# Another order for the closing steps of a graph attention layer on one Trainium2 core

## The chip, the cores and the metric

The kernel runs on one core of a Trainium2 chip. The metric is the device time of one execution in microseconds (us). For the kernel before it is 2030.86 us, the median of three runs (2030.07, 2030.86 and 2034.2). One further execution was profiled; it took 2036.32 us, of which its trace covers 2034.5 us.

## What is computed

The graph has 12500 nodes with 128 features and 200000 edges sorted by destination. Each destination keeps its 16 best edges.

```python
h = relu(layernorm(x))
score = einsum('md,md->m', (h @ W_Q.T)[dst], (h @ W_K.T)[src]) / sqrt(128) * exp(-edge_weight)
keep  = the 16 highest scores of each dst
alpha = softmax of the kept scores over the edges of one dst
agg   = segment_sum(alpha * (h[src] @ W_msg.T), dst)
out   = x + relu(h @ W_self.T + agg)
```

## The kernel before

**Groups.** The edges are cut into 112 groups of 14 chunks of 128 edges. Each group also looks one chunk into the next group, so it has 15 chunks; the last group, L = 111, has 9. All edges of a group point into a window of at most 128 destination nodes. A group goes through these steps, each a small function of the same name in the code:

- `q_to_edges(g, b)` (L596, TensorE): spreads the nodes' queries to the edges, block b of four chunks, in float32.
- `scores(g, b)` (L605, VectorE): one fused multiply and sum for each chunk, on the rows `hs` that GpSimd has gathered. `scores_in_slots` (L613, VectorE) puts the scores into 40 slots for each node.
- `slots_by_node` (L619, L621, TensorE), `slots_out` (L626, ScalarE), `node_by_slots` (L629, TensorE): the slots arrive with one node in each partition.
- `best` (L635 to L647, VectorE): nine small instructions that find the top 16 and leave them in `km`. `sum_of_exps` (L652, ScalarE) gives the softmax denominator.
- `kept_to_edges` (L664, TensorE): brings `km` back to the edges. `kept_on_edges` is `one_over_sum` (L657, L658, VectorE), `on_edges` (L670 to L677, VectorE: `up`, `mine`, `kept`) and `exps` (L681, ScalarE).
- `weights` (L685, L686, VectorE) writes the weight matrix `alz`.
- `sums(g, 0)` and `sums(g, 1)` (L696, TensorE): the weighted sums of the rows, the first half of the chunks and the rest: 7 and 8 chunks, 14 and 16 float32 matmul records. `sums_out` (L701, ScalarE) normalises them into `agn`; `sums_turned` and `sums_turned_out` (L704 on TensorE, L708 on ScalarE) transpose that.
- `products` (L711, L712, TensorE): the two weight products. `output` (L716, VectorE) applies relu and adds x. `store` writes the rows: through SyncE's queue (L722), and for the last four groups by an indirect DMA that GpSimd issues (L725).

**Order.** The order is written by hand. A schedule with no reordering is in force from the start of the loop over groups: every engine executes its own instructions in the order in which the program calls them, and waits on semaphores for those of other engines. Within the main loop the steps of six neighbouring groups are interleaved. The loop ends one iteration early, and a straight list of calls, the end's list, finishes the groups that are under way, L-5 to L. Only this list is changed.

**PSUM and buffers.** Three PSUM banks matter. `so` (tile `s` in the profile) holds four 128-column quarters: a transpose of h, the query, the transposed sums, and the result of `products`. `et` (tile `e`) holds slots and, inside the loop, the sums. Tile `a` holds the sums in the end's list. An engine's access to a bank waits for another engine's earlier access to the same bank, even if they touch different quarters: in the built program `sums_turned`, which writes one quarter of `so`, waits for the `output` called ahead of it, which reads another. A store waits for the stores before it, because all write `out`.

**Helpers of the end's list.** `turned(g)` is `sums_turned` and `sums_turned_out`; `all_slots(g)` is `slots_by_node` for three blocks and `slots_out`; `all_sums(g)` is both parts of `sums` and `sums_out`; `to_rows(g)` is `products`, `output` and `store`.

Of the kernel before, what the change touches and what calls it, by code (L numbers as in the profile page):

```python
# [20 lines left out]
P = 128  # L21
# [39 lines left out]
def bc(ap, n):  # L61

    return ap.unsqueeze(2).to_broadcast([ap.shape[0], ap.shape[1], n])


def upper(ap):

    return ap.bitcast(BF16).rearrange("p (n two) -> p n two", two=2)[:, :, 1]
# [8 lines left out]
def gnn_layer(  # L77
# [54 lines left out]
    def bank(tag, bufs):  # L132
        return psum.tile([P, 512], F32, tag=tag, bufs=bufs, name=tag)
# [376 lines left out]
    with tc.tile_pool(name="win", bufs=2) as win:  # L510
# [4 lines left out]
        def rows_of(g, j):  # L515
            return T[g]["hs"][:, j, :] if j < GC else T[g + 1]["hs"][:, 0, :]

        def start_of(g, row, most):
            return nc.values_load(row_i[0:1, row, g:g + 1], engines=[SP], min_val=0, max_val=most,
                                  skip_runtime_bounds_check_because="clamped above")  # L520
# [69 lines left out]
        def q_to_edges(g, b):  # L590
            j0, j1 = 4 * b, min(4 * b + 4, chunks[g])
            if j0 >= j1:
                return
            T[g]["pq", b] = pq = bank("q", 3)
            for j in range(j0, j1):
                nc.tensor.matmul(pq[:, (j - j0) * P:(j - j0 + 1) * P],  # L596
                                 lhsT=T[g]["to_e"][:, j * P:(j + 1) * P], rhs=T[g]["q"], start=True, stop=True)
# [30 lines left out]
        def node_by_slots(g):  # L628
            nc.tensor.transpose(et[:, 256:256 + KM + 1], T[g]["eT"], ident[0:KM + 1, 0:KM + 1])  # L629


        def best(g):
            pt = et[:, 256:256 + KM + 1]
            ell = win.tile([P, KM], F32, name="ell")
            nc.vector.tensor_scalar(ell, slots, pt[:, KM:KM + 1], NEG, op0=OP.is_ge, op1=OP.mult)  # L635
            nc.vector.tensor_add(ell, ell, pt[:, 0:KM])
            T[g]["v16"] = v16 = win.tile([P, TOPK], F32, name="v16")
            rest = win.tile([P, KM], F32, name="rest")
            nc.vector.max(v16[:, 0:8], ell)
            nc.vector.match_replace(rest, v16[:, 0:8], ell, NEG)  # L640
            nc.vector.max(v16[:, 8:16], rest)
            nc.vector.match_replace(rest, v16[:, 8:16], rest, NEG)
            T[g]["km"] = km = win.tile([P, KM + 3], F32, name="km")
            nc.vector.tensor_scalar(km[:, KM:KM + 1], v16[:, 0:1], FLOOR, -1.0, op0=OP.max, op1=OP.mult)
            nc.vector.tensor_tensor(km[:, 0:KM], rest, ell, op=OP.not_equal)
            for k in range(KM, KM + 2):
                nc.vector.tensor_sub(km[:, k + 1:k + 2], km[:, k:k + 1], upper(km[:, k:k + 1]))  # L647

        def sum_of_exps(g):
            T[g]["e16"] = win.tile([P, TOPK], F32, name="e16")  # L650
            T[g]["den"] = win.tile([P, 1], F32, name="den")
            nc.scalar.activation(T[g]["e16"], T[g]["v16"], AF.Exp, bias=T[g]["km"][:, KM:KM + 1],  # L652
                                 accum_out=T[g]["den"])

        def one_over_sum(g):
            T[g]["rden"] = rden = win.tile([P, 1], F32, name="rden", bufs=4)
            nc.vector.tensor_scalar(rden, T[g]["den"], 0.25, None, op0=OP.max)  # L657
            nc.vector.reciprocal(rden, rden)  # L658


        def kept_to_edges(g):
            T[g]["px"] = px = psum.tile([P, NJ + 1, 64], F32, tag="x", bufs=1, name="x")
            for j in range(chunks[g]):
                nc.tensor.matmul(px[:, j, 0:KM + 3], lhsT=upper(T[g]["to_e"][:, j * P:(j + 1) * P]),  # L664
                                 rhs=upper(T[g]["km"]), start=True, stop=True)
# [13 lines left out]
        def exps(g):  # L679
            n = chunks[g]  # L680
            nc.scalar.activation(T[g]["up"][:, 0:n], T[g]["up"][:, 0:n], AF.Exp)  # L681

        def weights(g):
            n, kept = chunks[g], T[g]["kept"]
            nc.vector.tensor_tensor(kept[:, 0:n], T[g]["up"][:, 0:n], kept[:, 0:n], op=OP.mult)  # L685
            nc.vector.tensor_tensor(alz[g % 2].rearrange("e (j w) -> e j w", w=WW + STEP)[:, 0:n, 0:WN],  # L686
                                    T[g]["ow"][:, 0:n, :], bc(kept[:, 0:n], WN), op=OP.mult)


        def sums(g, part, at=None):  # L690
            n = chunks[g]
            if part == 0:
                T[g]["pa"] = et[:, 384:384 + P] if at is None else at
            half = n // 2
            for j in range(half) if part == 0 else range(half, n):
                nc.tensor.matmul(T[g]["pa"], lhsT=alz[g % 2][:, WW * j + PRE:WW * j + PRE + P],  # L696
                                 rhs=rows_of(g, j), start=(j == 0), stop=(j == n - 1))

        def sums_out(g):
            T[g]["agn"] = win.tile([P, D], F32, name="agn")  # L700
            nc.scalar.activation(T[g]["agn"], T[g]["pa"], AF.Copy, scale=T[g]["rden"])  # L701

        def sums_turned(g):
            nc.tensor.transpose(so[:, 2 * P:3 * P], T[g]["agn"], ident)  # L704

        def sums_turned_out(g):
            T[g]["aggT"] = win.tile([P, P], F32, name="aggT")
            nc.scalar.copy(T[g]["aggT"], so[:, 2 * P:3 * P])  # L708

        def products(g):  # L710
            nc.tensor.matmul(so[:, 3 * P:4 * P], lhsT=T[g]["hT"], rhs=wselfT, start=True, stop=False)  # L711
            nc.tensor.matmul(so[:, 3 * P:4 * P], lhsT=T[g]["aggT"], rhs=wmsgT, start=False, stop=True)  # L712

        def output(g):
            T[g]["o"] = win.tile([P, D], F32, name="o")
            nc.vector.scalar_tensor_tensor(T[g]["o"], so[:, 3 * P:4 * P], 0.0, T[g]["x_t"],  # L716
                                           op0=OP.max, op1=OP.add)

        def store(g):

            if g < G - TAIL:
                nc.sync.dma_start(out[ds(start_of(g, 0, N - P), P), :], T[g]["o"])  # L722
            else:
                k = g - (G - TAIL)
                nc.gpsimd.indirect_dma_start(  # L725
                    out=out[:, :], out_offset=bass.IndirectOffsetOnAxis(ap=idxo[:, k:k + 1], axis=0),
                    in_=T[g]["o"], in_offset=None, bounds_check=N - 1, oob_is_err=False)
# [90 lines left out]
        L = G - 1  # L818
        blocks = -(-chunks[L] // 4)

        def turned(g):
            sums_turned(g)
            sums_turned_out(g)

        def all_sums(g):
            sums(g, 0, bank("a", 1)[:, 0:P])
            sums(g, 1)
            sums_out(g)

        def to_rows(g):  # L830
            products(g)
            output(g)
            store(g)

        def all_slots(g):
            for b in range(3):
                slots_by_node(g, b)
            slots_out(g)

        def kept_on_edges(g):  # L840
            one_over_sum(g)
            on_edges(g)
            exps(g)

        q_to_edges(L, 0)
        output(L - 5)
        store(L - 5)
        weights(L - 3)
        turned(L - 4)
        all_slots(L - 1)  # L850
# [2 lines left out]
        for b in range(1, blocks):  # L853
            q_to_edges(L, b)
        node_by_slots(L - 1)
        to_rows(L - 4)
        kept_to_edges(L - 2)
        all_sums(L - 3)
        scores(L, 0)
        kept_on_edges(L - 2)  # L860
        best(L - 1)
        sum_of_exps(L - 1)
        weights(L - 2)
        kept_to_edges(L - 1)
        scores(L, 1)
        turned(L - 3)
        all_sums(L - 2)
        for b in range(2, blocks):
            scores(L, b)
        scores_in_slots(L)  # L870
        all_slots(L)
        products(L - 3)
        node_by_slots(L)
        kept_on_edges(L - 1)
        weights(L - 1)
        output(L - 3)
        store(L - 3)
        best(L)
        sum_of_exps(L)
        turned(L - 2)  # L880
        pa = bank("a", 1)[:, 0:P]
        sums(L - 1, 0, pa)
        kept_to_edges(L)
        sums(L - 1, 1)
        sums_out(L - 1)
        to_rows(L - 2)
        kept_on_edges(L)
        weights(L)
        turned(L - 1)
        all_sums(L)  # L890
        to_rows(L - 1)
        turned(L)
        to_rows(L)
    assert not later
    order.close()

# [180 lines left out]
```

## Time and profile before

| What | Value |
|---|---|
| median of three runs | 2030.86 us |
| profiled execution | 2036.32 us |
| span of its trace | 2034.5 us |
| TensorE matmul busy | 1580.1 us (78%) |
| GpSimd busy | 1505.6 us (74%) |
| VectorE busy | 1284.9 us (63%) |
| ScalarE busy | 1021.7 us (50%) |
| mean granted TensorE clock | 0.915 |
| first steps that the change moves | 1991.75 us from the start |
| last gather issued (L176) | 1991.09 us |
| last store starts on GpSimd (L725) | 2021.33 us |

The shares of the whole span describe the main loop, 1990 us of it. The change concerns only the last 43 us, so the timeline of that stretch is what has to be read: one row for each instruction, or for a run of equal ones, with its start, its length, the engine, the line, the operands, and in brackets how long the engine sat idle ahead of it and which instruction ended that. PEld is TensorE's loading of weights, which overlaps its matmuls.

### The profile page before, as it was taken

What the parts mean: (1) busy time and instruction counts of PE and PEld (TensorE: products, weight loads), DVE (VectorE), ACT (ScalarE), POOL (GpSimd) and SP (SyncE); (2) the same over time, 40 slices, a digit from 0 to 9 for tenths busy, and PEclk for the clock granted to TensorE, in tenths of its full rate; (3) what the DMA queues carried; (4) which work ended last, traced back from release to release, by engine and by line L of the source; (5) the groups of instructions that cost most, each with busy time, mean ns of one, the idle gap of its engine ahead of it and who ended that gap; (6) DMA issues with size and microseconds to landing.
All of it is one profiled execution on the core that took longest, in us unless ns stands there. A gap on an engine that the chain in (4) does not pass through costs nothing. (4 is left out here: it accounts for less than half of the span.)

```text
span 2034.5 us, 42215 instructions
## 1 busy us (share of the span) xinstructions
PE 1580.1 (78%) x13800; PEld 1303.9 (64%) x13801; DVE 1284.9 (63%) x7017; ACT 1021.7 (50%) x2190; POOL 1505.6 (74%) x1580
## 2 busy tenths in 40 slices
PE   0268899977878787888878787778878787878785
PEld 0147777766666666666666666666666666666664
DVE  7568877756656666666666566666666665666653
ACT  5765566544444454454444445444544444545440
POOL 6777777777777777777777777777777777777772
PEclk9979999998889899998888899898988888989987
DMA  9522222222222222222222222222222222222220
GB/s 220 179 59 56 76 69 69 66 64 66 65 65 66 65 64 63 66 65 65 66 65 66 66 65 64 64 64 65 66 66 65 65 66 66 66 64 64 64 58 19
DMA packets 101472, 143.46 MB, mean 71 GB/s; under 512 B 31063, under 2 KB 74327, under 8 KB 100480
## 3 DMA queue, kind: packets, MB, share of 16 engines
q0 software_dynamic: 50144, 102.74, 19.9%
q1 hardware_dynamic: 51102, 37.99, 6.8%
q8 instruction: 108, 1.77, 0.4%
q14 instruction: 118, 0.97, 0.2%
HBM read 126.79 MB, written 14.40 MB: 69 GB/s over the span
## 5 line engine op out<-in xcount | busy, mean ns | idle before, releaser
L176 POOL DMA_INDIRECT hs<-h_tab,ix x1507 | 1436.4, 953 | 461.9 <-issue 304.6
L605 DVE SCALAR_TENSOR_TENSOR prod<-hs,dec_all,q 128x128 f32<-128x128 f32 x1674 | 507.6, 344 | 296.2 <-DMA hs<-h_tab,ix 256.8
L558 ACT ACTIVATE far<-a,minus 128x512 bf16<-128x512 f32 (+1 forms) x447 | 294.3, 658 | 530.8 <-PE a L556 523.7
L596 PE MATMUL q<-q,to_e 128*128 128x128 f32 x3348 | 512.4, 301 | 0.0
L596 PEld LDWEIGHTS q<-q,to_e 128*128 128x128 f32 x3348 | 482.6, 213 | 33.5 <-DVE prod L605 13.7
L696 PE MATMUL e<-hs,alz 128*128 128x128 f32 x3240 | 419.1, 282 | 0.0
L696 PEld LDWEIGHTS e<-hs,alz 128*128 128x128 f32 x3240 | 377.9, 192 | 26.9 <-issue 19.2
L581 ACT ACTIVATE aw<-a 128x400 bf16<-128x400 f32 x336 | 169.1, 503 | 314.3 <-PE a L579 314.3
L635 DVE TENSOR_SCALAR ell<-slots,e 128x40 f32<-128x40 f32 x112 | 28.1, 251 | 357.1 <-PE e L621 304.6
L704 PE MATMUL s<-ident,agn 128*128 128x128 f32 x112 | 38.3, 342 | 262.8 <-DVE kept L685 260.8
L563 ACT ACTIVATE to_e<-far 128x1920 f32<-128x1920 bf16 x112 | 201.4, 1798 | 3.5
L556 PE MATMUL a<-rel,ident 112*128 112x512 bf16 (+1 forms) x447 | 195.0, 436 | 8.2 <-ACT far L558 8.1
L704 PEld LDWEIGHTS s<-ident,agn 128*128 128x128 f32 x112 | 17.0, 152 | 279.0 <-issue 274.7
L621 PE MATMUL e<-opo,sl 128*41 128x40 f32 x3348 | 194.0, 233 | 0.0
L621 PEld LDWEIGHTS e<-opo,sl 128*41 128x41 f32 x3348 | 180.1, 147 | 12.3
L605 DVE DVE_READ_ACCUMULATOR prod<-hs,dec_all,q 128x1 f32 x1674 | 138.4, 83 | 0.0
L585 ACT ACTIVATE opo<-aw 128x1200 f32<-128x1200 bf16 x112 | 134.2, 1198 | 0.1
L191 DVE COPY ix<-idx_all 128x2 int32<-128x2 int32 x754 | 133.2, 192 | 0.0
L579 PE MATMUL a<-minus_at,pdT 32*128 32x400 bf16 x336 | 115.4, 343 | 19.3 <-ACT pdT L572 9.6
L664 PE MATMUL x<-km,to_e 128*128 128x43 bf16 x1674 | 61.1, 183 | 66.7 <-DVE km L647 66.0
L664 PEld LDWEIGHTS <-to_e 128*128 128x128 bf16 x1674 | 49.7, 97 | 98.3 <-DVE km L647 96.7
L613 DVE TENSOR_TENSOR sl<-opo,s 128x600 f32<-128x600 f32 x112 | 87.6, 782 | 4.0
(179 smaller groups left out, 1678.0 us busy)
## 6 DMA issues: line engine op xcount, KB each, us to landing
hs<-h_tab,ix POOLq DMA_INDIRECT x1507
h_r<-h_tab SPq DMA_DIRECT2D x112, 64.0 KB
x_t<-in_x_dram SPq DMA_DIRECT2D x108, 64.0 KB
out_dram<-o SPq DMA_DIRECT2D x108, 64.0 KB
xg<-in_x_dram SPq DMA_DIRECT2D x2, 1400.0 KB
h_tab<-xg SPq DMA_DIRECT2D x2, 1400.0 KB
xg<-in_x_dram SPq DMA_DIRECT2D x1, 1120.0 KB
h_tab<-xg SPq DMA_DIRECT2D x1, 1120.0 KB
```

The lines of the kernel that those rows point to most:

```text
L176: nc.gpsimd.indirect_dma_start(out=T[g]["hs"][:, j, :], out_offset=None, in_=table[0:N, :], in_offset=bass.IndirectOffsetOnAxis(ap=index(j ...
L191: nc.vector.tensor_copy(ix[:, j0:j1], idx_all[:, GC * g + j0:GC * g + j1])
L556: nc.tensor.matmul(pr[:, 0:n1 - n0], lhsT=upper(ident[0:RR, g:g + 1]).to_broadcast([RR, P]), rhs=rel[:, n0:n1], start=True, stop=True)
L558: nc.scalar.activation(T[g]["far"][:, n0:n1], pr[:, 0:n1 - n0], AF.Square, bias=minus)
L563: nc.scalar.activation(T[g]["to_e"][:, 0:n], T[g]["far"][:, 0:n], AF.Relu, bias=1.0, scale=-1.0)
L579: nc.tensor.matmul(pr[:, 0:400], lhsT=T[g]["pdT"], rhs=minus_at.rearrange("k w j s -> k (w j s)")[:, n0:n1], start=True, stop=True)
L581: nc.scalar.activation(T[g]["aw"][:, n0:n1], pr[:, 0:400], AF.Square)
L585: nc.scalar.activation(T[g]["opo"].rearrange("e w j s -> e (w j s)"), T[g]["aw"], AF.Relu, bias=1.0, scale=-1.0)
L596: nc.tensor.matmul(pq[:, (j - j0) * P:(j - j0 + 1) * P], lhsT=T[g]["to_e"][:, j * P:(j + 1) * P], rhs=T[g]["q"], start=True, stop=True)
L605: nc.vector.scalar_tensor_tensor(prod, rows_of(g, j), dec_all[:, c:c + 1], T[g]["pq", b][:, (j % 4) * P:(j % 4 + 1) * P], op0=OP.mult, op1 ...
L621: nc.tensor.matmul(et[0:KM + 1, STEP * j:STEP * j + WN], lhsT=sl1[g % 2][:, j, :], rhs=T[g]["ow"][:, j, :], start=False, stop=(j == n - 1))
L696: nc.tensor.matmul(T[g]["pa"], lhsT=alz[g % 2][:, WW * j + PRE:WW * j + PRE + P], rhs=rows_of(g, j), start=(j == 0), stop=(j == n - 1))
```

## The change

`all_sums` and `to_rows` are dissolved into their parts and the parts are called at other places of the end's list. No step is added or dropped. In the order of the list:

- `output(L-4)` and its store move from ahead of `scores(L, 0)` to behind `kept_on_edges(L-2)`.
- `sums_out(L-3)` moves behind `exps(L-2)` and `sum_of_exps(L-1)`.
- `sums(L-2, 1)` moves behind all of `slots_by_node(L)`; `sums_out(L-2)` moves behind `exps(L-1)`.
- `products(L-3)` moves behind `node_by_slots(L)`; `output(L-3)` and its store move from ahead of `best(L)` to behind it.
- `kept_on_edges(L)` moves ahead of `sums_out(L-1)`, `products(L-2)` and `output(L-2)`; the last comes behind `weights(L)`.

In the built program the number of waits differs by one, an extra instruction that only waits; everything ahead of the end's list is the same.

```diff
-        def all_sums(g):
+        def begun(g):
             sums(g, 0, bank("a", 1)[:, 0:P])
-            sums(g, 1)
-            sums_out(g)
-
-        def to_rows(g):
-            products(g)
-            output(g)
-            store(g)
...
+        def written(g):
+            output(g)
+            store(g)
+
         q_to_edges(L, 0)
-        output(L - 5)
-        store(L - 5)
+        written(L - 5)
         weights(L - 3)
         turned(L - 4)
         all_slots(L - 1)
...
         node_by_slots(L - 1)
-        to_rows(L - 4)
+        products(L - 4)
         kept_to_edges(L - 2)
-        all_sums(L - 3)
+        begun(L - 3)
+        sums(L - 3, 1)
         scores(L, 0)
         kept_on_edges(L - 2)
+        written(L - 4)
         best(L - 1)
         sum_of_exps(L - 1)
         weights(L - 2)
+        sums_out(L - 3)
         kept_to_edges(L - 1)
         scores(L, 1)
         turned(L - 3)
-        all_sums(L - 2)
+        begun(L - 2)
         for b in range(2, blocks):
             scores(L, b)
         scores_in_slots(L)
         all_slots(L)
-        products(L - 3)
+        sums(L - 2, 1)
         node_by_slots(L)
         kept_on_edges(L - 1)
+        sums_out(L - 2)
         weights(L - 1)
-        output(L - 3)
-        store(L - 3)
+        products(L - 3)
         best(L)
         sum_of_exps(L)
+        written(L - 3)
         turned(L - 2)
-        pa = bank("a", 1)[:, 0:P]
-        sums(L - 1, 0, pa)
+        begun(L - 1)
         kept_to_edges(L)
         sums(L - 1, 1)
+        kept_on_edges(L)
         sums_out(L - 1)
-        to_rows(L - 2)
-        kept_on_edges(L)
         weights(L)
+        products(L - 2)
+        written(L - 2)
         turned(L - 1)
-        all_sums(L)
-        to_rows(L - 1)
+        begun(L)
+        sums(L, 1)
+        sums_out(L)
+        products(L - 1)
+        written(L - 1)
         turned(L)
-        to_rows(L)
+        products(L)
+        written(L)
```

## The prediction

> **What bounds the kernel now.** I read first the chain of work that ended last, because the shares of the whole span (TensorE 78%, GpSimd 74%) belong to the main loop, which the change doesn't touch.
>
> ```profile
> 4 pieces in order of time: start us, us, what
> 2018.37 0.98 DMA out_dram<-o,idxo
> 2019.35 1.77 issue
> 2021.12 0.51 POOLq L904
> 2021.63 0.68 POOL out_dram L725
> ```
>
> The span ends with stores. The last one, store(L), starts 2.96 us after store(L-1) began, although its rows are there at 2020.14: it waits until the one before has landed. After its start at 2021.33 come 13.2 us in which no engine works; I take them as fixed. So the end is "start of store(L-1) + 2.96 + 13.2", and what counts is when output(L-1) is ready. Then I read the timeline of the last 45 us backwards from there.
>
> ```profile
> 2003.54 0.37 ACT L701 ACTIVATE agn<-a,rden 128x128 f32<-128x128 f32 x1 [5.13 <-PE a L696]
> 2004.47 0.26 ACT L626 COPY eT<-e 41x128 f32<-41x128 f32 x1 [0.57 <-PE e L621]
> 2004.88 0.17 DVE L685 TENSOR_TENSOR kept<-up,kept 128x15 f32<-128x15 f32 x1 [2.45 <-ACT up L681]
> 2005.99 0.24 DVE L635 TENSOR_SCALAR ell<-slots,e 128x40 f32<-128x40 f32 x1
> 2006.13 0.33 PE L704 MATMUL s<-ident,agn 128*128 128x128 f32 x1 [0.86 <-DVE o L716]
> 2010.90 0.29 DVE L716 SCALAR_TENSOR_TENSOR o<-s,x_t 128x128 f32<-128x128 f32 x1 [2.88 <-ACT agn L701]
> 2013.84 3.01 PE L696 MATMUL a<-hs,alz 128*128 128x128 f32 x18 [2.20 <-DVE alz L686]
> 2017.80 0.29 DVE L716 SCALAR_TENSOR_TENSOR o<-s,x_t 128x128 f32<-128x128 f32 x1 [4.01 <-PE s L712]
> ```
>
> From below: output(L-1) waits for products behind sums(L); sums(L) wait for the weights of L; these wait behind output(L-2) on VectorE, idle for 2.88 us. Above, VectorE stands 2.45 us for exps(L-1), which on ScalarE is queued behind sums_out(L-2) and eT(L), and so behind all 30 matmul records of sums(L-2). The last view is the busy time by microsecond; after the five engines stands the granted clock.
>
> ```profile
> 1996.00:1997.00 1.00, 0.00 (x0) 0.00 (x0) 0.90 (x9) 0.09 (x2) 0.00 (x0) 1.00 0.00 0
> 1999.00:2000.00 1.00, 1.00 (x7) 1.00 (x7) 0.96 (x7) 0.00 (x0) 0.00 (x0) 0.50 0.00 0
> 2009.00:2010.00 1.00, 1.00 (x12) 1.00 (x11) 0.00 (x0) 0.00 (x0) 0.00 (x0) 1.00 0.00 0
> 2016.00:2017.00 1.00, 1.00 (x6) 1.00 (x6) 0.00 (x0) 0.05 (x1) 0.00 (x0) 0.50 0.00 0
> ```
>
> After an idle stretch TensorE runs at half clock for about 3.4 us. At full clock 16 records of sums last 1.87 us (2008.32 to the next step at 2010.19), so 0.117 each; sums(L-2) ran at half clock from 1998.30 to 2001.47 and made its other 15 records by 2003.2 at that pace, so the first 15 cost 0.21 each.
>
> **The change part by part.** No step is added or removed, so every cost is a wait. Times are those of the trace; a step keeps its own length and its distance to the step that releases it. One distance isn't constant: from the end of a matmul to VectorE 0.04 to 0.10 us pass; I take 0.10.
>
> *output(L-4) off the front of scores(L,0).* VectorE ends `km` of L-2 at 1990.51 and idles 1.24 us for products(L-4). Now the four scores go at 1990.43 (the same step overlaps its forerunner by 0.08 at 1974.30) and last 4 x 0.27. Their rows are there: a gather issued at 1981.11 let its score go at 1983.67, 2.56 later, and the fourth was issued at 1984.86. Next late is kept_to_edges(L-2) on TensorE, which ends at 1992.09, so `up` starts at 1992.19 instead of 1993.29. output(L-4) then takes 0.20 behind `kept`. best(L-1) starts at 1994.40 (before 1995.30) and all that hangs on it comes 0.90 earlier: kept_to_edges(L-1) 1996.50, the weights of L-2 end 1997.34, scores(L,1) 1997.26. The store of L-4 is issued some 2.4 us later on SyncE; nothing but the end follows in that queue, and store(L-3) on GpSimd, which waits for it, comes some 11 us later. Cost 0.
>
> *sums_out(L-3) behind two exps on ScalarE.* It would start at 1996.34 instead of 1995.56 (behind sum_of_exps(L-1), at 1996.04 plus 0.30), ends at 1996.71, and turned(L-3), which stands behind kept_to_edges(L-1) on TensorE, goes at 1996.89. Cover 0.18 us, cost 0; without that cover sums(L-2) would slip by what is missing.
>
> *sums(L-2) in two.* First half: 1997.40, 14 x 0.117, to 1999.04. slots_by_node(L) then wait for the scores in slots: five scores from 1997.26 and L613 end them at 1999.25. Slots 1999.31 to 2000.21 (before 2003.54 to 2004.44), eT, exps(L-1) to 2000.61 (before 2004.84). The 2.45 us stall goes; next late is VectorE's own `kept` of L-1, until 2001.53. weights(L-1) start at 2001.64 instead of 2004.88: 3.24 earlier. The second half, 16 x 0.117, stands ahead of node_by_slots(L), which ends at 2002.26, beneath VectorE's weights: cover 0.3 us. best(L) starts at 2002.55 instead of 2005.99: 3.44 earlier.
>
> *output(L-3) behind best(L).* Here most is given back. turned(L-2) writes the bank that output(L-3) reads, and in the new program it waits for that output, now 2.04 us of best(L) later. Output 2004.55 to 2004.84, turned(L-2) at 2004.90: only 1.23 earlier than 2006.13, and TensorE, done with products(L-3) at about 2002.9 and with the weights of L-1 ready since 2002.63, idles 2 us. Behind it queue sums(L-1,0), kept_to_edges(L), sums(L-1,1).
>
> *kept_on_edges(L) ahead of output(L-2).* kept_to_edges(L) is no longer what `km` releases; it follows sums(L-1,0): 2005.06 + 1.64 = 2006.70 to 2007.10. `up` of L goes at 2007.20 (before 2011.37), 2.41 later its weights are done: 2009.61 (before 2013.78). VectorE waits about 2.4 us ahead of `up`, with nothing urgent behind it. products(L-2) end at 2009.42, output(L-2) 2009.54 to 2009.83, turned(L-1) 2009.89, sums(L) at 2010.05 instead of 2013.84: **3.79 earlier**. Both releasers of sums(L) now lie 0.3 us apart.
>
> *Behind that* all keeps its order. With sums(L) at full clock, 18 x 0.117 + 0.61 of products + 0.10 puts output(L-1) at 2012.87 instead of 2017.80; its store starts 0.57 later, at 2013.44 (store(L-2), at 2010.11, has landed by 2013.07), store(L) at 2016.40: a gain of **4.93**.
>
> **The clock, and a rule.** That sum needs full clock throughout. The Trainium skill, "TensorE: Matmul & The Clock Gate", section "Why this matters for your kernels", asks only that no gap between bursts exceeds about 3 us. By it the new gap of 2 us would be harmless: 4.93. The trace disagrees: the clock fell at 1998.12 after a gap of 1.88 us. Its changes (1984.47, 1991.25, 1998.12, 2001.47, 2015.19) are multiples of about 3.41 us apart, as the same page's window of 3413 ns has it; at full clock, windows with 1.3 to 1.5 us of TensorE work led to half clock, one with 2.5 did not. On this grid the new order has 2.27 us of work in the window to 1998.12, which I take as kept at full clock, but 1.4 in that to 2004.94. So I take the row: half clock from 2004.94 to 2008.35. sums(L-1,0) then last 14 x 0.21, kept_to_edges(L) ends at 2008.50, its `up` starts at 2008.60, the weights of L end at 2011.01, output(L-2) at 2011.23, sums(L) at 2011.45; then full clock: output(L-1) 2014.27, store(L-1) 2014.84, store(L) 2017.80. **Gain 3.53 us**: the profiled 2036.32 becomes 2032.8. Its overhead over the median (5.5 us) is not explained by the trace; I take the same gain from the median: 2030.86 - 3.5 = **2027.4**.
>
> **The rivals.** (a) No half clock in the new gap: 4.93, so 2025.9. For it: the windows are placed anew in each execution. (b) The before of the timed runs lacks the two half-clock stretches of this trace. They cost 15 x (0.21 - 0.117) = 1.4 to 1.6 us in sums(L-2), and 1.1 in sums(L) and its products; without both, store(L) of before is at 2018.6 and the gain against an undisturbed after is 2.2: 2028.7. For it: the runs lie 4 us apart. (c) The other side: slots_by_node(L) don't come earlier, since sl(L) hangs on a VectorE chain of some 30 instructions. Then two things that the change puts in line cost their price: 16 records ahead of node_by_slots(L) and best(L) ahead of turned(L-2). Slots at 2003.54 give best(L) 2006.54, turned(L-2) 2008.89, and sums(L), 5.15 behind it, 2014.04: this decides from slots later than about 2003.3. The price is 0.2 at full clock, 1.7 with the 16 records at half clock (16 x 0.093), 3.1 with those of L-1 too; I take 1.7: 2032.6. Against it: nothing of before holds that VectorE chain for four us. (d) The end hangs on something else than the stores, the fixed 13.2 us included: 2030.9. Against it: the chain ends in store(L).
>
> **How the numbers follow.** A measurement of this kernel can tell about 0.2% from no change, 4.06 us. Forecast 40 in 100 (its spread 3.0 to 4.5, of it 12 beyond 0.2%), (a) 27, all beyond, (b) 18, (c) 10, of which 5 beyond once run spread is added, (d) 5. Faster by over 0.2%: 0.39; within: 28 + 18 + 5 + 5 = 0.56; slower: 0.05. The range runs from 2025.2 (4.9 and 0.8 of run spread) to 2030.2, which leaves out (c), (d) and some of the rest.
>
> **What would show it.** Right: weights(L-1) start some 3.2 us earlier in the trace's end with no 2.45 us stall ahead; turned(L-2) waits for output(L-3) with TensorE idle about 2 us; `up` of L waits for kept_to_edges(L) and the weights of L end 2.7 to 4.2 us earlier; store(L) still 2.96 behind store(L-1). Wrong: a store chain that starts late, sums(L-2,0) held by sums_out(L-3), or a granted clock of 0.5 at sums(L).

## The result and the profile after

| | before | after |
|---|---|---|
| median (lowest to highest) of 22 runs each | 2031.65 us (2028.43 to 2035.7) | 2029.7 us (2026.17 to 2032.23) |
| ratio after / before, 95% interval | | 0.9987 (0.9981 to 0.9993) |
| profiled execution, span of its trace | 2036.32, 2034.5 | 2031.5, 2029.7 |
| mean granted TensorE clock | 0.915 | 0.921 |

The new order is faster by 0.13%: the ratio stands for 2.6 us, with an interval of 1.4 to 3.9 us, and the medians lie 1.95 us apart. The two profiled executions lie 4.82 us apart. The end of the chain of waits of after is built as it was before, 4.6 us earlier:

```profile
2013.77 0.98 DMA out_dram<-o,idxo
2014.75 1.78 issue
2016.53 0.51 POOLq L908
2017.03 0.69 POOL out_dram L725
```

The last store still starts 2.97 us behind the one before it. The timeline of after, with the rows that answer to those of before:

```profile
1997.36 0.31 PE L704 MATMUL s<-ident,agn 128*128 128x128 f32 x1
...
2000.62 2.05 PE L696 MATMUL a<-hs,alz 128*128 128x128 f32 x16
...
2002.10 0.17 DVE L685 TENSOR_TENSOR kept<-up,kept 128x15 f32<-128x15 f32 x1
...
2003.01 0.24 DVE L635 TENSOR_SCALAR ell<-slots,e 128x40 f32<-128x40 f32 x1
...
2005.44 0.30 PE L704 MATMUL s<-ident,agn 128*128 128x128 f32 x1 [1.94 <-DVE rden L657]
...
2007.56 0.19 DVE L670 TENSOR_REDUCE up<-x 128x9 f32<-128x27 f32 x1 [2.01 <-PE x L664]
...
2010.49 2.17 PE L696 MATMUL a<-hs,alz 128*128 128x128 f32 x18
...
2013.20 0.29 DVE L716 SCALAR_TENSOR_TENSOR o<-s,x_t 128x128 f32<-128x128 f32 x1 [3.00 <-ACT agn L701]
```

VectorE no longer waits ahead of the weights of L-1 (2002.10; 2.45 us of waiting before) and TensorE no longer 2.20 us ahead of sums(L), which ran in 2.17 us instead of 3.01. Two new waits stand in their place: TensorE's 1.94 us ahead of turned(L-2), and VectorE's 2.01 us for kept_to_edges(L). By the microsecond, with the granted clock behind the five engines:

```profile
1996.00:1997.00 1.00, 0.03 (x1) 0.03 (x2) 0.93 (x8) 0.49 (x3) 0.00 (x0) 1.00 0.10 28
1999.00:2000.00 1.00, 1.00 (x13) 0.80 (x12) 0.93 (x6) 0.00 (x0) 0.00 (x0) 1.00 0.00 0
2004.00:2005.00 1.00, 0.00 (x0) 0.00 (x0) 0.90 (x8) 0.29 (x2) 0.00 (x0) 1.00 0.00 0
```

TensorE has two idle stretches here too, and the clock held at 1.00 through both, from 1990.23 to beyond the last matmul (it fell at 2017.53).

**Cutting the end in two.** The start of best(L-2), its first VectorE instruction at L635, comes before anything that the change moves. It lay between 1985.88 and 1990.24 us in the ten traces of this study that were taken at the usual pace, whatever the kernel. That spread of 4.4 us has nothing to do with the change, so I measure from there: the *front*, from the start of best(L-2) to that of best(L-1), and the *back*, from there to the start of the last store. In before they are 1988.46 to 1995.30 and on to 2021.33: 6.84 and 26.03 us; in after 1989.37 to 1994.87 to 2016.74: 5.50 and 21.87. After the last store's start 13.2 and 13.0 us follow. So the profiled gain of 4.8 us is 1.34 in the front, 4.16 in the back, 0.2 behind it, less 0.91 by which after happened to arrive later.

### The profile page after: what moved, and what is told of

It is laid out like the page before. It is cut to its first block, busy times and chain, and to the rows that moved or that the text cites. A ratio compares the mean times of both kernels' runs of the same rounds, so it can differ in the third digit from the quotient of the medians.

```text
span 2029.7 us, 42216 instructions
## 1 busy us (share of the span) xinstructions
PE 1569.0 (77%) x13800; PEld 1294.4 (64%) x13801; DVE 1286.2 (63%) x7017; ACT 1023.5 (50%) x2190; POOL 1510.5 (74%) x1580
## 5 line engine op out<-in xcount | busy, mean ns | idle before, releaser
L176 POOL DMA_INDIRECT hs<-h_tab,ix x1507 | 1440.8, 956 | 459.6 <-issue 290.4
L635 DVE TENSOR_SCALAR ell<-slots,e 128x40 f32<-128x40 f32 x112 | 28.3, 253 | 350.7 <-PE e L621 291.9
L621 PE MATMUL e<-opo,sl 128*41 128x40 f32 x3348 | 189.6, 230 | 0.0
L621 PEld LDWEIGHTS e<-opo,sl 128*41 128x41 f32 x3348 | 175.9, 144 | 12.0
```

Source lines behind the costliest of these rows:

```text
L176: nc.gpsimd.indirect_dma_start(out=T[g]["hs"][:, j, :], out_offset=None, in_=table[0:N, :], in_offset=bass.IndirectOffsetOnAxis(ap=index(j ...
L621: nc.tensor.matmul(et[0:KM + 1, STEP * j:STEP * j + WN], lhsT=sl1[g % 2][:, j, :], rhs=T[g]["ow"][:, j, :], start=False, stop=(j == n - 1))
```

## The experiments

Theory 1: the prediction's waits are right, and its size was wrong, because the half-clock stretches of the trace of before come in some executions and not in others. The rivals: half clock is always there and the gain is eaten elsewhere; the change acts through one part alone.

All of them in one table. "Half clock" is where the granted clock was 0.50 between the start of best(L-2) and the last matmul ("front 2.8": the first 2.8 us of the front); the ratio is to before, on the same chip.

| kernel | front | back | half clock | ratio (95%) |
|---|---|---|---|---|
| before | 6.84 | 26.03 | front 2.8; sums(L-2); sums(L) | |
| before_b | 5.56 | 23.36 | none | |
| before_busy | 7.00 | 23.34 | front 3.2 | 0.9995 (0.9985 to 1.0005) |
| only_split | 5.56 | 25.42 | sums(L) | 0.9997 (0.9988 to 1.0006) |
| only_split_b | 6.43 | 25.41 | front 1.8; sums(L) | 0.9993 (0.9984 to 1.0002) |
| only_last | 6.52 | 22.15 | front 2.0; sums(L-2) | 0.998 (0.997 to 0.9989) |
| last_busy | 6.92 | 20.86 | front 3.0 | 0.9982 (0.9973 to 0.9992) |
| after | 5.50 | 21.87 | front 0.9 | 0.9987 (0.9981 to 0.9993) |
| after_b | 5.51 | 21.87 | none | 0.9999 (0.999 to 1.0008) |
| after_busy | 5.94 | 21.85 | front 2.9 | 0.9983 (0.9974 to 0.9992) |
| out3_first | 5.98 | 20.56 | front 3.1 | 0.9976 (0.9965 to 0.9986) |
| own_bank | 5.51 | 21.00 | none | 0.9993 (0.9984 to 1.0002) |
| own_bank_b | 5.99 | 21.20 | front 3.1 | 0.9979 (0.997 to 0.9988) |
| early_out3 | 5.52 | 20.15 | front 1.8 | 0.997 (0.9959 to 0.998) |

Where the clock agrees, the back repeats to 0.02 us (21.85, 21.87, 21.87; 23.34, 23.36), bar own_bank's 0.2. That is a far finer gauge than the times, whose intervals are 2 to 4 us wide.

### Filling TensorE's gaps: before_busy and after_busy

Matmuls that nobody reads, into a free bank; before_busy gets seven (14 records) and eight, after_busy five and seven.

```diff
+        def busy(n):
+            pq = bank("q", 3)
+            for j in range(n):
+                nc.tensor.matmul(pq[:, 0:P], lhsT=ident, rhs=wselfT, start=True, stop=True)
...
 (before_busy)
+        busy(7)
         kept_to_edges(L - 1)
...
+        busy(8)
         all_sums(L)
...
 (after_busy)
+        busy(5)
         kept_to_edges(L - 1)
...
+        busy(7)
         turned(L - 2)
```

> The order of before, with matmuls added whose results nobody reads: 7 float32 products (14 records, about 1.6 us at full clock) in TensorE's idle gap ahead of kept_to_edges(L-1), and 8 in the gap ahead of sums(L). The tail is counted from the start of best(L-2) to the start of the last store: 32.9 us in the trace of before, 27.4 in that of after. Theory 1 (part of the tail is TensorE at half clock after an idle gap, and whether a gap meets a whole window differs from execution to execution): no half clock from sums(L-2) on, a tail of 30.0 to 30.6 us, and a time 0.7 to 1.6 us under before, since only some executions of before have the two stretches. Theory 2 (the clock doesn't set the tail, the waits alone do): a tail of 32.5 to 33 us and no change of time.

> The order of after with 5 unread float32 products ahead of kept_to_edges(L-1) and 7 in the 1.9 us gap ahead of turned(L-2). Theory 1: no half clock from sums(L-2) on, a tail of 27.3 to 27.8 us as in the trace of after, a time 0 to 0.8 us under after, 2 to 3.5 under before. Theory 2: the same tail, no change against after; the two differ in before_busy.

The timeline of before_busy:

```profile
1993.77 1.73 PE L848 MATMUL q<-wselfT,ident 128*128 128x128 f32 x14
...
1996.71 3.62 PE L696 MATMUL a<-hs,alz 128*128 128x128 f32 x30 [0.20 <-DVE alz L686]
...
2001.77 0.17 DVE L685 TENSOR_TENSOR kept<-up,kept 128x15 f32<-128x15 f32 x1 [0.93 <-ACT up L681]
...
2010.72 2.27 PE L696 MATMUL a<-hs,alz 128*128 128x128 f32 x18 [0.41 <-DVE alz L686]
```

With the gaps filled, sums(L-2) took 3.62 us instead of 5.14, VectorE's stall ahead of the weights of L-1 fell from 2.45 to 0.93 us, and the back from 26.03 to 23.34. So 2.69 us of the back of before were half clock, by no other change than work for TensorE. In after_busy a like filling did nothing (21.85 beside 21.87): after's gaps cost no clock in its trace. In the times before_busy can't be told from before (0.6 us between the medians, where I had expected 0.7 to 1.6). If all timed runs of before had both stretches, its ratio would be 0.9987, which its interval just holds; if none had, 1.0.

### The two kernels again: before_b and after_b

> The kernel before once more, for another profile. Theory 1: the two stretches of half clock lie elsewhere or are missing: a tail of 30.3 us without them, 31.5 with one, 32.9 with both. Theory 2: 32.9 us again.

> The kernel after once more, for another profile and the times on one chip with the others. Theory 1: a tail of 27.3 us at full clock, up to 28.8 where the 1.9 us gap ahead of turned(L-2) meets a window of the clock; the part ahead of the tail 1986 to 1990 us, and its spread, the same program in every run, explains most of the spread of the times. Theory 2 (the tail alone varies): the same lead as in the trace of after, 1989.4 us, and another tail.

In that set of runs every kernel took some 3140 us (see the last section), but the end of the list ran at its usual pace. The timeline of before_b:

```profile
3103.11 3.62 PE L696 MATMUL a<-hs,alz 128*128 128x128 f32 x30 [0.20 <-DVE alz L686]
...
3108.16 0.17 DVE L685 TENSOR_TENSOR kept<-up,kept 128x15 f32<-128x15 f32 x1 [0.93 <-ACT up L681]
...
3117.13 2.27 PE L696 MATMUL a<-hs,alz 128*128 128x128 f32 x18 [2.20 <-DVE alz L686]
```

Unfilled, and still full clock: before can do without its half-clock stretches. Front and back then are 28.92 us (1.4 less than the 30.3 that I had expected, because this front too ran at full clock) and after_b's 27.38: **1.54 us** is what the change saves when the clock never falls. The times of after_b (ratio 0.9999) do not resolve that.

The traces also tell why the stretches were missing. In each trace the clock changes only at steps of 3.41 us, but this grid lies elsewhere in each: its first step behind the start of best(L-2) came after 2.83 us in before and after 0.59 in before_b. In before, the 2.20 us gap ahead of sums(L) lay whole in one window of the grid (2011.77 to 2015.19), which left 1.35 us of TensorE work in it, and the clock fell. In before_b a step of the grid cut the gap at 3115.62; the two windows kept 2.18 and 1.90 us of work, and the clock held. Over all 14 traces, 87 windows at full clock lie whole between the start of best(L-2) and the last matmul. Six of them held 1.35 to 1.62 us of TensorE work, and five of these were followed by half clock; the other 81 held 1.80 us or more, and none was. The border isn't sharp: a window of before_b in which the matmuls end fell with 1.83 us of work.

### The last part alone: only_last and last_busy

Before, with nothing changed but the order behind kept_to_edges(L); last_busy is the same with busy(7) ahead of kept_to_edges(L-1).

```diff
         sums(L - 1, 1)
-        sums_out(L - 1)
-        to_rows(L - 2)
         kept_on_edges(L)
+        sums_out(L - 1)
         weights(L)
+        to_rows(L - 2)
         turned(L - 1)
```

> The order of before with one part of the change alone: kept_on_edges(L) and weights(L) ahead of sums_out(L-1), products(L-2) and output(L-2). Theory 1: up of L starts right behind kept_to_edges(L) instead of 2.9 us later, so sums(L) come 2.4 us earlier with no idle gap worth a window ahead: a tail of 30.4 us where sums(L-2) meet half clock, 28.8 where they don't, a time 1.5 to 2.8 us under before. Rival (the early part of the change brings the gain, because the last part only swaps one wait for another): a tail of 32 us or more and no change of time.

> only_last (of the change, only kept_on_edges(L) ahead of sums_out(L-1), products(L-2) and output(L-2)) with seven matmuls that nobody reads ahead of kept_to_edges(L-1), so that TensorE has work in the gap after which sums(L-2) ran at half clock. It tells what the other parts of the change are worth once the clock holds. Theory 1 (nothing but insurance against half clock: they bring output(L-3) behind best(L), which costs 1.2 us, for stalls that are short at full clock): turned(L-2) 14.9 us behind the start of best(L-2) at full clock, 16.3 with a half-clock front as in before_busy, the last store 11.5 us later: tail 26.4 or 27.8, in either case about 1 us less than the kernel after with the same front (27.4 at full clock). Rival (the other parts gain at full clock too): tail 28.4 or more, 1 us above the kernel after. sums(L-2) at 3.6 us instead of 4.92. Ratio to before 0.9975 to 0.999, no better to be told from only_last by the time alone.

The timeline of only_last:

```profile
1998.89 4.92 PE L696 MATMUL a<-hs,alz 128*128 128x128 f32 x30
...
2005.25 0.17 DVE L685 TENSOR_TENSOR kept<-up,kept 128x15 f32<-128x15 f32 x1 [2.23 <-ACT up L681]
...
2011.81 2.17 PE L696 MATMUL a<-hs,alz 128*128 128x128 f32 x18
```

And that of last_busy:

```profile
2000.14 3.62 PE L696 MATMUL a<-hs,alz 128*128 128x128 f32 x30 [0.20 <-DVE alz L686]
...
2005.20 0.17 DVE L685 TENSOR_TENSOR kept<-up,kept 128x15 f32<-128x15 f32 x1 [0.93 <-ACT up L681]
...
2006.45 0.33 PE L704 MATMUL s<-ident,agn 128*128 128x128 f32 x1 [0.87 <-DVE o L716]
```

only_last ended 1.7 us sooner than I had expected for a run with half clock in sums(L-2) (28.67 against 30.4). I had not counted that sums(L), with no wait ahead of it, then keeps full clock, which is 1.25 us of it (2.71 us from its start to output(L-1), against 3.96 in before); a shorter front (6.52 against 6.84) and a shorter sums(L-2) (4.92 against 5.14) make up the rest. With the gap filled the back is 20.86: **in the back, at full clock, the last part alone saves 2.50 us (23.36 - 20.86), a whole microsecond more than the entire change** (23.36 - 21.87 = 1.49). The sum of front and back, 27.78, came out as expected for a half-clock front; but the kernel after with such a front (after_busy) has 27.79, so "1 us less than the kernel after" failed for the whole and holds for the back only. What makes up for it is the front: with half clock for some 3 us of it, it takes 6.84 to 7.00 us in before's order and 5.94 to 5.99 in after's. At full clock it is 5.56 against 5.51: moving output(L-4) is worth 1 us in the one case and nothing in the other.

### The split alone: only_split and its repeat

Before with sums(L-2) split around the last slots, sums_out(L-2) behind exps(L-1), and products(L-3) behind node_by_slots(L).

```diff
-        all_sums(L - 2)
+        sums(L - 2, 0, bank("a", 1)[:, 0:P])
...
-        products(L - 3)
+        sums(L - 2, 1)
         node_by_slots(L)
         kept_on_edges(L - 1)
+        sums_out(L - 2)
         weights(L - 1)
+        products(L - 3)
         output(L - 3)
```

> The order of before with the part on sums(L-2) alone: its second half behind slots_by_node(L), sums_out(L-2) behind exps(L-1), products(L-3) behind node_by_slots(L); output(L-3) stays ahead of best(L), kept_on_edges(L) behind output(L-2). Theory 1: weights(L-1) start 1.9 to 2.4 us earlier, turned(L-2) 1.4 to 1.9 us, and all behind by the same, as the last wait (weights of L behind output(L-2)) is unchanged: a tail of 29.9 to 31.5 us, the more where gaps meet half clock, against 32.9. Rival (the last part alone brings the gain, and this one moves only where VectorE waits): a tail of 32.3 us or more.

> A repeat of only_split, to see its tail without a half-clock stretch in sums(L): theory 1 (splitting sums(L-2) alone brings nothing at full clock, since output(L-3) no longer hides and best(L) isn't earlier than VectorE's own work allows): tail 28.7 to 29.2, beside 28.92 of before at full clock. Rival (it brings the 0.8 us by which weights(L-1) come earlier): 28.1. A half-clock stretch in sums(L-2) would cost it nothing to 0.5, in sums(L) 2. Ratio to before 0.999 to 1.0.

The timeline of only_split_b:

```profile
2001.12 0.29 DVE L716 SCALAR_TENSOR_TENSOR o<-s,x_t 128x128 f32<-128x128 f32 x1 [0.44 <-PE s L712]
...
2009.18 4.21 PE L696 MATMUL a<-hs,alz 128*128 128x128 f32 x18 [2.20 <-DVE alz L686]
...
2014.34 0.29 DVE L716 SCALAR_TENSOR_TENSOR o<-s,x_t 128x128 f32<-128x128 f32 x1 [5.21 <-PE s L712]
```

In both executions sums(L) fell to half clock behind TensorE's wait of 2.20 us. From its start to output(L-1) 5.16 us passed, in before_b 2.81 (3117.13 to 3119.94). Without these 2.35 us the back would by this estimate be 23.06, 0.3 below before's 23.36; no execution of only_split showed it at full clock. The prediction had weights(L-1) 3.24 us earlier, 0.90 of it by the front and 2.34 by the split. Counted from the start of best(L-1), they come after 9.58 us in before, 8.05 in before_b and 7.23 in both runs of only_split: the split brings 0.82, and 1.53 were the stall of the half-clock run. VectorE now waits for products(L-3) instead (0.44 us).

### What output(L-3) behind best(L) costs: out3_first

After, with output(L-3) and its store ahead of best(L) again.

```diff
         products(L - 3)
+        written(L - 3)
         best(L)
         sum_of_exps(L)
-        written(L - 3)
         turned(L - 2)
```

> The order of after with output(L-3) and its store ahead of best(L) again. Theory 1 (the new wait of turned(L-2) for output(L-3) gives back part of the gain): output(L-3) is ready 0.6 us after the weights of L-1, best(L) starts 0.8 us later than in after, but turned(L-2) goes 1.5 us earlier, kept_to_edges(L), then released by km, 1.2 us earlier; a tail of 26.1 to 26.5 us, a time about 1.2 us under after. Rival (best(L) on the path that sets the end, since kept_to_edges(L) needs km): the 0.8 us are paid and nothing won, a tail of 28.2 us.

The timeline of out3_first:

```profile
2001.90 0.29 DVE L716 SCALAR_TENSOR_TENSOR o<-s,x_t 128x128 f32<-128x128 f32 x1 [0.45 <-PE s L712]
...
2002.34 0.30 PE L704 MATMUL s<-ident,agn 128*128 128x128 f32 x1 [0.48 <-DVE ell L635]
...
2004.63 0.19 DVE L670 TENSOR_REDUCE up<-x 128x9 f32<-128x27 f32 x1
```

VectorE waits 0.45 us for products(L-3), and in exchange TensorE's wait ahead of turned(L-2) shrinks from 1.94 to 0.48 us and VectorE's 2.01 us for kept_to_edges(L) is gone. The back is 20.56, 1.31 below after's; with its half-clock front the whole is 26.54, at the upper end of the 26.1 to 26.5 expected. So the change's back splits up at full clock: -2.50 (last part), +1.31 (output(L-3) behind best(L)), and -0.30 for the rest (20.86 to 20.56). Together -1.49. The sum closes by the way it is made; what supports it is that the estimate from only_split gave the same 0.30.

### The bank as the cause of that wait: own_bank and its repeat

After, with products and output of the last four groups in a bank of their own, so that turned(L-2) doesn't write where output(L-3) reads.

```diff
-            nc.tensor.matmul(so[:, 3 * P:4 * P], lhsT=T[g]["hT"], rhs=wselfT, start=True, stop=False)
-            nc.tensor.matmul(so[:, 3 * P:4 * P], lhsT=T[g]["aggT"], rhs=wmsgT, start=False, stop=True)
+            ro = T[g]["ro"] = bank("q", 3)[:, 0:P] if g > G - 5 else so[:, 3 * P:4 * P]; nc.tensor.matmul(ro, lhsT=T[g]["hT"], rhs=wselfT, start=True, stop=False)
+            nc.tensor.matmul(T[g]["ro"], lhsT=T[g]["aggT"], rhs=wmsgT, start=False, stop=True)
...
-            nc.vector.scalar_tensor_tensor(T[g]["o"], so[:, 3 * P:4 * P], 0.0, T[g]["x_t"],
+            nc.vector.scalar_tensor_tensor(T[g]["o"], T[g]["ro"], 0.0, T[g]["x_t"],
```

> The order of after, unchanged; products and output of the last four groups use a PSUM bank of their own, one that the queries no longer need. So turned(L-2) need not wait for output(L-3), which still stands behind best(L). Theory 1 (that wait is what gives part of the gain back): turned(L-2) goes 2.0 us earlier, right behind products(L-3); kept_to_edges(L) is then released by km, 2.0 us earlier than in after; a tail (start of best(L-2) to start of the last store) of 24.8 to 25.6 us against 27.4, a time 2 us under after. Rival (best(L) is the path, the wait lies beside it): a tail of 27 us or more.

> A repeat of own_bank, to time it beside the others on one chip. Tail again 26.3 to 26.7 at full clock (theory: the stores bind it), 0.9 less than the kernel after; ratio to before 0.9975 to 0.9985 where the chip runs the main loop at its usual pace, 0.999 to 1.0 where it doesn't.

The wait went as expected: turned(L-2) ran 13.98 us after the start of best(L-2), in after_b 16.08. But the end came only 0.87 us earlier instead of some 2. GpSimd's timeline of own_bank, the four stores:

```profile
3114.22 1.01 POOL L725 DMA_INDIRECT out_dram<-o,idxo  x1 [67.08 <-DVE up L673]
3117.28 1.00 POOL L725 DMA_INDIRECT out_dram<-o,idxo  x1 [2.05 <-DVE o L716]
3120.28 0.98 POOL L725 DMA_INDIRECT out_dram<-o,idxo  x1 [2.00 <-issue]
3123.96 0.98 POOL L725 DMA_INDIRECT out_dram<-o,idxo  x1 [2.70 <-DVEq L908]
```

The rows of L-1 and L were written by VectorE at 3118.88 and 3120.12, 1.4 and 3.8 us ahead of their stores. All four stores now stand in one line at 3 us or more, and that line starts with store(L-3), which the change had put late. The repeat had a back of 21.20 and a ratio of 0.9979, inside what was expected, except that its 27.19 from best(L-2) on include a half-clock front.

### The store chain started earlier: early_out3

own_bank with products(L-3) ahead of the last slots and output(L-3) ahead of best(L):

```diff
         begun(L - 2)
+        products(L - 3)
         for b in range(2, blocks):
...
-        products(L - 3)
+        written(L - 3)
         best(L)
         sum_of_exps(L)
-        written(L - 3)
         turned(L - 2)
```

> own_bank (products and output of the last four groups in a bank of their own) with products(L-3) moved ahead of slots_by_node(L) and output(L-3) with its store moved ahead of best(L). It tells whether the tail of own_bank (26.51 us from the start of best(L-2) to the start of the last store) is now set by the chain of stores. Theory 1 (yes): store(L-3) starts about 2.1 us earlier, the four stores follow at about 3 us, bound again by output(L-1): tail 25.0 to 25.3 at full clock, with VectorE without a wait from best(L-2) to the weights of L. Rival: the two products ahead of the slots push exps(L-1) and node_by_slots(L) back by their 0.6 us and VectorE waits: tail 25.7 to 26.0. Second rival: the stores' spacing isn't a wait for the store before but the transfer's own pace or issue, and the last store stays where it was: 26.5. Of the time, if the tail decides: 0.9985 of the kernel after, about 3 us less than it at the same lead.

GpSimd's timeline of early_out3:

```profile
2000.66 1.01 POOL L725 DMA_INDIRECT out_dram<-o,idxo  x1 [11.29 <-DVE v L639]
2005.33 1.00 POOL L725 DMA_INDIRECT out_dram<-o,idxo  x1 [3.65 <-DVE o L716]
2008.33 0.98 POOL L725 DMA_INDIRECT out_dram<-o,idxo  x1 [2.00 <-DVE o L716]
2011.55 0.98 POOL L725 DMA_INDIRECT out_dram<-o,idxo  x1 [2.24 <-issue]
```

Now store(L-3) has 4.67 us of room, and store(L-2) starts 0.57 behind its own output (2004.76) rather than behind the store before. The back is 20.15, 0.85 to 1.05 below own_bank's, although output(L-1) came 0.34 us later behind best(L-1) than in own_bank (16.26 against 15.92). So the store chain did bind there. The total of 25.67 lies above the 25.0 to 25.3 that I had expected: VectorE has not one wait between best(L-2) and output(L-1), so the 0.29 us of output(L-3) in its line are paid in full where I had counted 0.1, and the last store came 3.22 behind the one before. It has the lowest ratio here, 0.997 (0.9959 to 0.998), with a median of 2026.74 us. Its lead over after's 0.9987 is 0.17%; the two were timed beside different runs of before, and the upper end of the one interval lies just under the lower end of the other. From out3_first and own_bank_b the times don't tell it apart.

## Why the prediction was right and wrong

The measured 2029.7 us lie in the range, near its upper end, and the change is faster by less than 0.2%; to a change of at most that size the prediction had given 0.56. Its row of 3.5 us is inside the interval of 1.4 to 3.9, near the far end. Step by step, in us from the start of best(L-2); the predicted column is the sum at full clock, and with the half clock in the new gap the last two rows were 22.99 and 29.34:

| step | before | predicted, full clock | after |
|---|---|---|---|
| best(L-1) starts | 6.84 | 5.94 | 5.50 |
| weights(L-1) start | 16.42 | 13.18 | 12.73 |
| best(L) starts | 17.53 | 14.09 | 13.64 |
| turned(L-2) | 17.67 | 16.44 | 16.07 |
| sums(L) start | 25.38 | 21.59 | 21.12 |
| last store | 32.87 | 27.94 | 27.37 |

- **The waits were right.** Each step is 0.4 to 0.6 us earlier than written, and nearly all of that is the front, which left half clock 0.9 us after the start of best(L-2) in after, 2.8 us in before. With half clock as long there as in the trace that the prediction used, three kernels with after's front give 5.94 to 5.99, beside 5.94 predicted. sums_out(L-3) cost nothing (turned(L-3) at 1997.36 without a wait), nor did the second half of sums(L-2) (best(L) at 2003.01 without a wait).
- **output(L-3) behind best(L) gives back**: predicted 2 us of TensorE idle, measured 1.94, and out3_first prices it at 1.31 us of the back.
- **The half clock in the new gap failed to come.** "Half clock from 2004.94 to 2008.35" was to cost 1.4 us. Neither after nor after_b shows it, and filling the gap gained nothing. The rule by work in a window held; the placing was wrong. In both traces a step of the grid cut the 1.94 us of idle: in after at 2003.88 (3.03 and 1.85 us of work on its two sides), in after_b at 3115.16 (3.09 and 1.80). I had carried the grid of one execution over to another, though I had named as rival (a) that windows are placed anew. Whole in one window, the gap would leave at most 1.47 us of work by estimate (3.41 - 1.94), an amount at which the clock mostly fell, so other executions of after may pay this cost; two traces can't say how many. That the wrong placing lowered the forecast from 4.93 to 3.53, towards the measured gain, was luck.
- **The term that was mis-sized** is the half clock of before, in the step "I take the same gain from the median". Its size was right in the profiled execution: 2.69 us in the back (predicted 1.4 to 1.6 in sums(L-2) and 1.1 in sums(L)). But before_b had none of it, so one trace's cost is not the median's. The gain is 1.54 us without half clock anywhere, about 2.5 with it in the front of both (30.34 of before_busy less 27.79 of after_busy), and 5.5 in the two traces. The medians' 1.95 and the ratio's 2.6 lie on both sides of the 2.2 of rival (b), which the prediction gave 18 in 100; the interval holds the 1.54 and the 2.5 alike and leaves out 5.5.
- **Open:** how often the timed executions of before and after meet half clock, since only the profiled ones show where the clock fell. Unfilled orders with TensorE's 2.2 us wait ahead of sums(L) ran it at half clock in three of four traces (before, only_split, only_split_b; not before_b); the orders without that wait never did, in nine traces. That the change insures against half clock there is thus likely, and its share of the median is not measured.

## What to carry to other kernels

Before summing up what an edit saves, ask of each stall on the path whether it is the order's or the clock's: a stall behind matmuls at half clock can shrink by itself in another execution, as VectorE's did from 2.45 us in before to 0.93 in before_b. Try the parts of a reordering one by one; here one part carried 2.50 us and another took 1.31 back, because a consumer was moved behind nine instructions while a writer of the same bank waited for it. When a wait has been removed, look at the next serial line (here the stores, 3 us each) before expecting the whole of the wait as a gain.

## What else the runs showed of the hardware

**The same steps arrive up to 4.4 us apart** at the start of best(L-2), some 1988 us into the execution, though the program ahead of it is the same in all ten traces. The timed runs of after alone span 6.06 us, so a gain of 1.5 us in the tail is read from the trace better than from times.

**A set of runs at another pace.** The kernels before_b, after_b, only_split and own_bank ran together and took some 3140 us, before as well; runs under the same chip number somewhat later took 2032. The groups of the page of after_b (line, engine, operation and tile, count; busy time and mean ns of one; idle time ahead and what ended most of it):

```profile
L176 POOL DMA_INDIRECT hs<-h_tab,ix x1507 | 1450.8, 963 | 1516.0 <-PE e L696 595.9
L605 DVE SCALAR_TENSOR_TENSOR prod<-hs,dec_all,q 128x128 f32<-128x128 f32 x1674 | 483.2, 345 | 391.7 <-remote 330.3
```

The gathers take GpSimd no longer each (963 ns, in after 956), but it stands idle 1516 us ahead of them instead of 459.6, the mean transfer rate is 46 GB/s instead of 71, and the mean granted clock 0.743. The closing steps ran at their usual pace (the back of after_b is 21.87 us, as in after). What held the gathers up stays open.

**Stores.** A store by GpSimd starts 0.57 us behind its `output`, the first of the four 1.12 us behind (2005.01 to 2006.13 in after, the same in out3_first and early_out3). Where a store waits for the one before it, they start 2.95 to 3.06 us apart, but the last one came 3.68, 3.90 and 3.22 us behind its forerunner in own_bank, own_bank_b and early_out3. Why is open.
